# The down projection of a LUT feed-forward block in two parts of its contracted axis, with the partial rows kept in DRAM between them

## The chip, the cores and the metric

One core of one Trainium2 chip runs the whole program: a pre-norm block of attention over features and a feed-forward layer, in float32, on 2 x 2048 tokens of width 512. The metric is the device time of one execution in microseconds (us). The kernel before takes 1078.72 us (median of 3 runs, 1078.33 to 1079.13). The execution that the profiler recorded took 1078.93 us, and its instructions span 1077.2 us.

## The reference, cut to what matters

```python
x = x + attention(_layernorm(x), Wq, Wk, Wv, Wo)      # over the feature axis
x = x + ffn(_layernorm(x), lut, gate_idx, up_idx, down_idx)

def ffn(x, lut, gate_idx, up_idx, down_idx):          # HIDDEN 512, INTER 1376, LUT 16
    gate = einsum('bsh,oh->bso', x, lut[gate_idx])
    up = einsum('bsh,oh->bso', x, lut[up_idx])
    h = silu(gate) * up
    return einsum('bsh,oh->bso', h, lut[down_idx])
```

The weights of the feed-forward layer do not exist as numbers: each is an index from 0 to 15 into a table of 16 values, and the kernel has to look them up.

## The kernel before, in words

**Tiling.** The 4096 tokens are 8 chunks (NCH) of 512. The 1376 hidden features are 11 blocks (NFT), ten of 128 rows and one of 96. All large products go through a seven-product scheme (Strassen's, in Winograd's form): instead of eight products of half-size blocks, seven, for which VectorE first makes sums of the operands (S1, S2, S4 and S3 on one side, T1, T2, T4 and T3 on the other).

**Stages.** From 0 to about 295 us the program does the attention; from there to 804 us the gate and up products, in units of a block f and a pair of chunks p (`GateUp`), whose hidden rows go to DRAM (`hd`); from 804 us to the end the down products.

**Looking up.** A job (`Job`) turns a tile of 128x512 indices into weights on VectorE: four small operations on the bits of the index, eight `tensor_scalar` that pick between two table values (L278), and seven `copy_predicated` that merge them (L290). ScalarE first casts the indices to 16 bits (L252), and POOL loads them (L355 for down). There are 33 jobs, eleven each for gate, up and down. The list `jobs` has their order. They are not run in one go: `pump(us)` emits the next operations for about so many us, and the units call it through `between()` after each product, so that lookups and the rest of VectorE's work alternate. In the kernel before, all eleven down jobs are interleaved with the gate and up jobs and end before the last block of gate and up. Their results stay in one tile `wd`.

**between().** After each product of a unit, `between()` first takes an entry of the list `todo`, if there is one (sums to make, or other small work) and pumps 0.3 us of lookups; if there is none, it emits the sums that the next pair of blocks needs (`sums_left`, tiles `lc` and `lb`, as soon as its weights are there); otherwise it pumps `pace[0]` us.

**Down before.** For each chunk c, `Hidden(c)` loads all hidden rows of the chunk from DRAM: five pairs of blocks of 512 KB each (`h`, L1245) and the last block of 192 KB (`hr`, L1251), on SyncE's queue. VectorE makes the 21 sums of the chunk. Each chunk then has two units `Down(h, jj)`, for the two halves of its left rows. A unit has seven products: `a1`, `c1`, the `a4` of the unit before, `a2`, `c2`, `b`, `a3`; its own `a4` is the third product of the following unit. Each product adds up five pairs, and four of the seven also the last block: 39 matmuls of 128x256 a unit. After `a1`, `c1` and `a2` ScalarE copies the PSUM tile out (L1332, L1339, L1345), since the same PSUM tile is accumulated further; VectorE adds all seven results into rows `r` (L136). The rows start as the residual: the normed rows come back from DRAM (`xn_back`, two loads of 256 KB a unit, L1290) and ScalarE undoes the norm into `r` (`rows()`, two activations, L225). Finished rows are stored to the output.

**What sets the order around the change.** The order on PE, ScalarE, VectorE and SyncE is the order of the program's text; each engine runs its instructions in that order, and waits in it. Four orders matter. SyncE has, at the start of a chunk: the store of the last rows of the chunk before (L1362, which waits for VectorE's add after `a3`), then the loads of the next chunk's `h`, then the two `xn_back` loads for this chunk's second unit, then the store after `a4` (L1324). ScalarE has the two activations of L225 for a unit after the copies of the unit before and ahead of the unit's own copies. VectorE has, in the second unit of a chunk, the sums of the next chunk between the seven adds. PE's third product of a unit (`a4` of the unit before) needs the add after `a3`, its `a2` needs ScalarE's copy after `a1`.

Pools are stacks: `gub` (indices and lookup tiles) is released before the last block of gate and up, and the down tiles take its room.

Of the kernel before, what the change touches and what calls it, by code (L numbers as in the profile page):

```python
# [46 lines left out]
F32 = mybir.dt.float32  # L50
# [17 lines left out]
def tile_attn_ffn(  # L68
# [44 lines left out]
    lut_x = const.tile([P, NLUT // 2], I32, tag="lutx", name="lut_x")  # L113
    eps_sb = const.tile([P, 1], F32, tag="eps", name="eps_sb")
    lut_i = lut_sb.bitcast(I32)
    wd = wdp.tile([P, NFT, E], F32, tag="wd", name="wd")
    nd = dram.tile([NCH, P, KB, J, P], F32, tag="nd", name="nd")
    xnd = dram.tile([NCH, P, KB, J, P], F32, tag="xnd", name="xnd")
    hd = dram.tile([NCH, NFT, P, CH], F32, tag="hd", name="hd")


# [2 lines left out]
    def room(tag, name):  # L124
        return keep.tile([P, J, E], F32, tag=tag, name=name)
# [6 lines left out]
    def sub(dest, a, b):  # L132
        nc.vector.tensor_tensor(dest, a, b, ALU.subtract)
# [218 lines left out]
    def down_job(i):  # L352
        f0, rows = FT[i]
        return Job(
            f"wd{i}", rows, E, lambda queue, idx: queue.dma_start(idx, down_idx[f0 : f0 + rows, :]),  # L355
            lambda: wd[:rows, i, :], lambda: iter(()), lambda: True,
        )


    jobs = [job(f) for f in range(2) for job in (gate_job, up_job)]  # L360
    jobs += [down_job(i) for i in range(4)]
    for f in range(2, NFT - 1, 2):
        jobs += [gate_job(f), up_job(f), gate_job(f + 1), up_job(f + 1)]
        jobs += [down_job(i) for i in {2: (4,), 4: (5, 6), 6: (7,), 8: (8, 9)}[f]]
    jobs += [gate_job(NFT - 1), up_job(NFT - 1), down_job(NFT - 1)]
    assert len(jobs) == 3 * NFT

    def looked_up():
# [596 lines left out]
    def there(f):  # L965
        return f in gw and len(gw[f].shape) == 3 and f in uw
# [217 lines left out]
    todo = []  # L1184

    def between():
        if todo:
            todo.pop(0)()
            pump(0.3)
        elif sums_of and there(sums_of[0] | 1):  # L1190
            for op in sums_left(sums_of.pop()):
                op()
        else:
            pump(pace[0])

# [17 lines left out]
        late(i, **w)  # L1213


    wd_ops = []
    hps = {}

    def down_sums(pool):
        ops = []  # L1220
        for i in range(NPAIR):
            t = pool.tile([P, 3, H], F32, tag=f"t{i}", name=f"dT_{i}")
            t1, t2, t4 = (t[:, q, :] for q in range(3))
            b11, b12 = wd[:, 2 * i, :H], wd[:, 2 * i, H:]
            b21, b22 = wd[:, 2 * i + 1, :H], wd[:, 2 * i + 1, H:]
            wd_ops.append(
                {"11": b11, "T3": b12, "21": b21, "22": b22, "T1": t1, "T2": t2, "T4": t4}
            )
            ops += [
                lambda v=(t1, b12, b11): sub(*v), lambda v=(t2, b22, t1): sub(*v),  # L1230
                lambda v=(b12, b22, b12): sub(*v), lambda v=(t4, b21, t2): sub(*v),
            ]
        return ops

    class Hidden:


        ROOMS = [("a0", "x0", "a1"), ("a2", "a3", "x3")]

        def __init__(self, c):  # L1240
            self.c = c
            self.tiles = []
            for i in range(NPAIR):
                h = hps[c % 2].tile([P, 2, CH], F32, tag=f"h{i}", name=f"h_{c}_{i}")
                nc.sync.dma_start(h, hd[c, 2 * i : 2 * i + 2].rearrange("o p t -> p o t"))  # L1245
                self.tiles.append(h)

        def rest_of(self):
            c, rows = self.c, FT[NFT - 1][1]
            self.hr = hps[c % 2].tile([P, CH], F32, tag="hr", name=f"hr_{c}")[:rows]  # L1250
            nc.sync.dma_start(self.hr, hd[c, NFT - 1, :rows, :])  # L1251

        def sums(self):
            c, rows = self.c, FT[NFT - 1][1]
            places = []
            for tag in self.ROOMS[c % 2]:
                t = room(tag, f"hs_{c}_{tag}").rearrange("p j (q h) -> p (j q) h", h=H)
                places += [t[:, 0:3, :], t[:, 3:6, :]]
            self.pairs, ops = [], []
            for h, s in zip(self.tiles, places):  # L1260
                a11, a21 = h[:, 0, :H], h[:, 0, H:]
                a12, a22 = h[:, 1, :H], h[:, 1, H:]
                s1, s2, s4 = (s[:, q, :] for q in range(3))
                self.pairs.append(
                    {"11": a11, "12": a12, "S3": a21, "22": a22, "S1": s1, "S2": s2, "S4": s4}
                )
                ops += [
                    lambda v=(s1, a21, a22): add(*v), lambda v=(s2, s1, a11): sub(*v),
                    lambda v=(a21, a11, a21): sub(*v), lambda v=(s4, a12, s2): sub(*v),
                ]  # L1270
            h, s = self.hr, places[NPAIR][:rows, 0, :]
            self.rest = {"1": h[:, :H], "2": h[:, H:], "12": s}
            ops.append(lambda v=(s, h[:, :H], h[:, H:]): sub(*v))
            return ops

    class Down:


        def __init__(self, h, jj):
            self.h, self.c, self.jj, self.name = h, h.c, jj, f"{h.c}_{jj}"  # L1280
            self.r = []
            if h.c % 2 == 0 and jj == 0:
                for q in range(2):
                    rows_in[q] = room(f"x{1 + q}", f"r_{h.c}_{q}")
            if not normed_in:
                normed_in.append(room("sq0", "xn_back"))
            self.n = [normed_in[0][:, 2 * jj + i, :] for i in range(2)]
            self.n = [t.rearrange("p (i e) -> p i e", i=KB) for t in self.n]
            for i, j in enumerate((jj, 2 + jj)):
                nc.sync.dma_start(self.n[i], xnd[h.c][:, :, j, :])  # L1290
                self.r.append(rows_in[h.c % 2][:, 2 * jj + i, :])

        def rows(self):

            for i, j in enumerate((self.jj, 2 + self.jj)):
                ln2[self.c].undone(j, self.n[i], self.r[i])

        def at(self, a):
            return a[:, self.jj * P : (self.jj + 1) * P]

        def pairs(self, a, b):
            return [(self.at(self.h.pairs[i][a]), wd_ops[i][b]) for i in range(NPAIR)]

        def rest(self, a, b):
            rows = FT[NFT - 1][1]
            w = wd[:rows, NFT - 1, :]
            return [(self.at(self.h.rest[a]), w[:, :H] if b == "1" else w[:, H:])]

        def view(self, tag):
# [8 lines left out]

        def store_half(self, e):

            o, r = outr[self.c][:, self.jj, :], self.r[0]
            if self.c < NCH - 1 or self.jj == 0:
                if e:
                    nc.sync.dma_start(o, r)  # L1324
            else:
                nc.sync.dma_start(o[:, e * H : (e + 1) * H], r[:, e * H : (e + 1) * H])
# [31 lines left out]
        def a3(self):  # L1358

            mm(self.a, self.pairs("S1", "T1") + self.rest("2", "2"), False)  # L1360
            self.onto(1, 1, self.a)
            nc.sync.dma_start(outr[self.c][:, 2 + self.jj, :], self.r[1])  # L1362

        def a4(self):
            mm(self.a, self.pairs("S4", "22") + self.rest("12", "2"), False)
# [22 lines left out]
    for (f, p), following in zip(units, units[1:] + [(NFT, 0)]):  # L1388
# [8 lines left out]
        if f == NFT - 1 and p == 0:  # L1397
            assert not todo and next(lookup, None) is None
            x2p.release()
            gub.release()  # L1400
            for name in ("hp0", "dT"):
                hps[name] = tc.alloc_tile_pool(
                    name=name, bufs=1, side="right", reuse_waits="tile"
                )
            hps[0] = hps["hp0"]
            h = Hidden(0)
            todo += by_two(sums_last(f) + down_sums(hps["dT"]))
        if f == NFT - 1 and p == 1:
            h.rest_of()
            todo += by_two(h.sums())  # L1410
        if f == NFT - 1 and p == 3:
            units = [Down(h, 0)]
# [13 lines left out]
        op()  # L1426
    todo.clear()

    dtp = hps["dt"] = None
    for c in range(NCH):  # L1430
        nxt = None
        for jj in range(2):
            if c == 0 and jj == 0:
                units[0].rows()
                line.flush()
                ffn.release()
                wgu.release()
                hps[1] = tc.alloc_tile_pool(name="hp1", bufs=1, reuse_waits="tile")
                dtp = tc.alloc_tile_pool(name="dt", bufs=6, reuse_waits="tile")
            if jj == 0 and c + 1 < NCH:  # L1440
                nxt = Hidden(c + 1)
                nxt.rest_of()
            u = units.pop(0)
            if jj == 0:
                units.append(Down(h, 1))
            elif nxt is not None:
                units.append(Down(nxt, 0))
                todo += by_two(nxt.sums())
            line.run(u, final=nxt is None and jj == 1)
            if units:  # L1450
                units[0].rows()
        for op in todo:
            op()
        todo.clear()
        h = nxt
    line.flush()
    for pool in (dtp, hps[1], keep, hps["dT"], hps["hp0"]):
        pool.release()
    fps.release()

# [47 lines left out]
```

## Time and profile before

| stage (us from the start) | length | PE busy | VectorE busy | ScalarE busy | DMA |
|---|---|---|---|---|---|
| attention, to 295 | 295 | 291.6 | 244.1 | 138.0 | 42 to 272 GB/s |
| gate and up, 295 to 804 | 509 | 507.4 | 424.0 | 181.3 | 105 to 166 GB/s |
| down, 804 to the end | 273 | 269.6 | 99.8 | 41.2 | 134 GB/s |
| whole span 1077.2 | | 1068.6 (99%) | 768.0 (71%) | 360.5 (33%) | 143 GB/s |

The profiled execution took 1078.93 us for its span of 1077.2 us; 1.7 us lie outside. PE is TensorE's matmuls, PEld its weight loads, DVE VectorE, ACT ScalarE, SP SyncE; "SPq" in a row is a DMA being issued from SyncE. A matmul in float32 is recorded twice, so "x10" of PE is five matmuls. The timeline gives the start, the length, the instruction, and in brackets the idle time before it and what ended that.

### The profile page before, as it was taken

How to read it: one execution, taken by the hardware profiler on the slowest of the kernel's cores; microseconds unless marked ns; L12 is line 12 of the kernel's file. 1: busy time of each engine (PE TensorE's matmuls, PEld its weight loads, DVE VectorE, ACT ScalarE, POOL GpSimd, SP SyncE). 2: the span in 40 equal slices, each digit the busy share in tenths (PEclk: the TensorE clock that was granted, in tenths of full speed). 3: DMA queues.
4: the chain of work that ended last, by engine and by line, in shares of the span. 5: the costliest groups of instructions: out<-in, count | busy, mean ns of one | idle time of the engine just before them, and what ended most of it. 6: DMA issues, size and time to landing. Idle time of an engine off the chain costs nothing.

```text
span 1077.2 us, 10786 instructions
## 1 busy us (share of the span) xinstructions
PE 1068.6 (99%) x3426; PEld 641.0 (60%) x3426; DVE 768.0 (71%) x1660; ACT 360.5 (33%) x671; POOL 79.7 (7%) x118
## 2 busy tenths in 40 slices
PE   8999999999999999999999999999999999999998
PEld 5668886444444444444444444444348888888887
DVE  7878777889885889899899999985643334433341
ACT  4652432555632223333343343334221111111110
POOL 0000000011110000220120031012000000000000
PEclk9999999999999999999999999999999999999999
DMA  8750313589561244664574466456424545345421
GB/s 344 232 166 12 87 38 91 136 215 235 156 172 43 107 167 156 166 157 137 141 159 139 164 153 152 141 155 136 154 60 163 183 157 167 98 128 183 156 67 40
DMA packets 107769, 153.89 MB, mean 143 GB/s; under 512 B 16432, under 2 KB 52528, under 8 KB 106816
## 3 DMA queue, kind: packets, MB, share of 16 engines
q1 hardware_dynamic: 75744, 107.51, 30.6%
q0 software_dynamic: 11904, 28.91, 13.8%
q10 hardware_dynamic: 20064, 16.78, 4.9%
q8 instruction: 27, 0.44, 0.2%
q14 instruction: 30, 0.25, 0.1%
HBM read 89.73 MB, written 63.44 MB: 142 GB/s over the span
## 4 chain that ended last, share of the span: by engine, by line
PE 90%; DVE 4%; ACT 2%; DMA 1%; issue 1%; ACTq 1%; SPq 0%; DVEq 0%
PE a_g L997 27%; PE a_d L997 14%; PE y L770 10%; PE c_g L997 9%; PE c_d L997 7%; PE b_d L997 4%; PE x_g L997 4%; PE z_g L997 4%; PE b_g L997 2%; PE ea_t L607 1%; PE ea_p L607 1%; PE ea_m L607 1%; DVE st_a L154 1%; PE gp L454 1%; DMA x<-in_x_dram 1%
## 5 line engine op out<-in xcount | busy, mean ns | idle before, releaser
L770 PE MATMUL y<-m,nT 128*128 128x512 f32 x256 | 110.2, 592 | 0.0
L770 PEld LDWEIGHTS y<-m,nT 128*128 128x128 f32 x256 | 48.6, 190 | 60.4 <-issue 57.4
L997 PE MATMUL a_g<-xb,s 128*128 128x512 f32 (+1 forms) x176 | 82.7, 592 | 0.0
L997 PE MATMUL a_g<-xb,wg 128*128 128x512 f32 (+1 forms) x176 | 82.7, 592 | 0.0
L997 PE MATMUL c_g<-xb,wu 128*128 128x512 f32 (+1 forms) x176 | 82.7, 592 | 0.0
L997 PE MATMUL a_g<-xT_a,s 128*128 128x512 f32 (+1 forms) x176 | 82.7, 592 | 0.0
L454 PE MATMUL gp<-xn_a 128*128 128x128 f32 (+3 forms) x256 | 70.1, 434 | 1.7 <-DVE xn_a L177 0.9
L997 PE MATMUL a_g<-xT_sq,s 128*128 128x512 f32 (+1 forms) x132 | 62.0, 592 | 0.0
L454 PEld LDWEIGHTS gp<-xn_a 128*128 128x128 f32 x256 | 43.9, 190 | 28.5 <-issue 15.1
L997 PEld LDWEIGHTS a_g<-xb,s 128*128 128x128 f32 (+1 forms) x176 | 33.0, 188 | 42.5 <-issue 39.6
L997 PEld LDWEIGHTS a_g<-xT_a,s 128*128 128x128 f32 (+1 forms) x176 | 33.0, 188 | 42.5 <-issue 41.8
L997 PEld LDWEIGHTS c_g<-xb,wu 128*128 128x128 f32 (+1 forms) x176 | 33.0, 188 | 42.5 <-issue 42.3
L997 PEld LDWEIGHTS a_g<-xb,wg 128*128 128x128 f32 (+1 forms) x176 | 33.0, 188 | 42.5 <-issue 42.3
L290 DVE COPY_PREDICATED wd<-b_wd,wd 128x512 f32<-128x512 int16 (+1 forms) x77 | 56.4, 732 | 1.8
L997 PE MATMUL a_d<-dT,hs_a 128*128 128x256 f32 x224 | 56.2, 379 | 0.0
L136 DVE TENSOR_TENSOR r<-r,a_d 128x256 f32<-128x256 f32 x32 | 13.5, 421 | 53.7 <-PE a_d L997 53.7
L136 DVE TENSOR_TENSOR u<-c_g,u 128x512 f32<-128x512 f32 (+1 forms) x28 | 19.3, 690 | 37.5 <-PE c_g L997 31.7
L997 PEld LDWEIGHTS a_d<-dT,hs_a 128*128 128x128 f32 x224 | 42.4, 189 | 6.0
L278 DVE TENSOR_SCALAR wd<-idx_wd,lut_x,lut_sb 128x512 int32<-128x512 int32 (+1 forms) x88 | 44.5, 538 | 0.0
L997 PEld LDWEIGHTS a_g<-xT_sq,s 128*128 128x128 f32 (+1 forms) x132 | 24.8, 188 | 31.9 <-issue 31.4
L1128 ACT ACTIVATE h<-a_g 128x512 f32<-128x512 f32 (+1 forms) x44 | 26.2, 597 | 43.9 <-PE a_g L997 43.9
L1110 ACT ACTIVATE h<-h 128x512 f32<-128x512 f32 x24 | 15.1, 631 | 77.0 <-DVE h L136 77.0
(316 smaller groups left out, 2033.8 us busy)
## 6 DMA issues: line engine op xcount, KB each, us to landing
hd<-h SPq DMA_DIRECT2D x80, 256.0 KB, 2.2
h<-hd SPq DMA_DIRECT2D x40, 512.0 KB, 6.4
nl<-nd SPq DMA_DIRECT2D x32, 256.0 KB, 5.7
xnd<-xn_f ACTq DMA_DIRECT2D x16, 512.0 KB, 6.0
fl<-xnd POOLq DMA_DIRECT2D x32, 256.0 KB, 6.3
xn_back<-xnd SPq DMA_DIRECT2D x32, 256.0 KB, 4.4
out_dram<-r SPq DMA_DIRECT2D x31, 256.0 KB, 2.9
x<-in_x_dram SPq DMA_DIRECT2D x7, 1024.0 KB, 14.1
```

What stands on the lines that cost most here:

```text
L136: nc.vector.tensor_tensor(dest, a, b, ALU.add)
L154: nc.vector.bn_stats(st, block)
L278: vec.tensor_scalar(dest.bitcast(I32), idx, lut_x[:rows, k : k + 1], lut_i[:rows, at : at + 1], ALU.bitwise_and, ALU.bitwise_xor,)
L290: vec.copy_predicated(dest, masks[level - 1], t)
L454: nc.tensor.matmul(gp[b][i][:, i * P :], xn[:, i, j % 2, :], xn[:, i:, j % 2, :], start=c % CPB == 0 and j == 0, stop=c % CPB == CPB - 1 a ...
L607: nc.tensor.matmul(ps[:, m, :], self.a[a][:, k, m * P : (m + 1) * P], self.b[b][:, k, :], start=first and m == k == 0, stop=k == 1, skip_g ...
L770: nc.tensor.matmul(ys[k], nTs[k][:, i, :], m[:, i, :], start=(i == 0), stop=(i == KB - 1))
L997: nc.tensor.matmul(ps, lhsT, rhs, start=first and i == 0, stop=i == len(pairs) - 1, skip_group_check=not first,)
L1110: nc.scalar.activation(h0, self.p1 if self.role in (None, 3) else h0, AF.Silu)
L1128: nc.scalar.activation(self.h1, self.a, AF.Silu)
```

## The change

The down stage is run twice over all eight chunks. Part 0 takes the first three pairs of blocks of the contracted axis (K1 = 6 blocks), starts its rows from the residual as before, and stores the rows to a DRAM tensor `rd`. Part 1 takes the two other pairs and the last block, loads its rows from `rd` straight into `r`, and stores to the output. There are 32 units instead of 16: in part 0 a product adds up three matmuls (21 a unit), in part 1 two or three (18 a unit). The number of matmuls is the same; VectorE's adds grow from 112 to 224 and ScalarE's copies after `a1`, `c1`, `a2` from 48 to 96. The `h` loads are the same bytes in total, three pairs a chunk in part 0, two and `hr` in part 1.

The weights of the last five down blocks (6 to 10) get a tile `wd2` of their own, which exists only once the gate and up tiles are released. Their five jobs stand at the end of the list and run in part 0, pumped with `pace[0] = 0.75`; what is left of them would be emitted ahead of part 0's last chunk, where the sums of these weights are made too. `gub` stays until the end. Lookups in gate and up thus are five fewer, and the later gate and up jobs come earlier.

`between()` now emits `sums_left` before it takes from `todo`.

```diff
+    K1 = 6
+    wd = wdp.tile([P, K1, E], F32, tag="wd", name="wd")
+    rd = dram.tile([NCH, P, J, E], F32, tag="rd", name="rd")
...
-            lambda: wd[:rows, i, :], lambda: iter(()), lambda: True,
+            lambda: wd_block(i)[:rows], lambda: iter(()), lambda: i < K1 or wd2,
...
+    def wd_block(i):
+        return wd[:, i, :] if i < K1 else wd2[0][:, i - K1, :]
...
-        jobs += [down_job(i) for i in {2: (4,), 4: (5, 6), 6: (7,), 8: (8, 9)}[f]]
-    jobs += [gate_job(NFT - 1), up_job(NFT - 1), down_job(NFT - 1)]
+        jobs += [down_job(i) for i in {2: (4,), 4: (5,)}.get(f, ())]
+    jobs += [gate_job(NFT - 1), up_job(NFT - 1), *(down_job(i) for i in range(K1, NFT))]
...
     def between():
-        if todo:
+        if sums_of and there(sums_of[0] | 1):
+            for op in sums_left(sums_of.pop()):
+                op()
+        elif todo:
             todo.pop(0)()
             pump(0.3)
-        elif sums_of and there(sums_of[0] | 1):
-            for op in sums_left(sums_of.pop()):
-                op()
         else:
             pump(pace[0])
...
+    PARTS = [range(0, K1 // 2), range(K1 // 2, NPAIR)]
...
+            self.to = outr[h.c] if self.part else rd[h.c]
             for i, j in enumerate((jj, 2 + jj)):
-                nc.sync.dma_start(self.n[i], xnd[h.c][:, :, j, :])
                 self.r.append(rows_in[h.c % 2][:, 2 * jj + i, :])
+                if self.part:
+                    nc.sync.dma_start(self.r[i], rd[h.c][:, j, :])
+                else:
+                    nc.sync.dma_start(self.n[i], xnd[h.c][:, :, j, :])
...
-            for i, j in enumerate((self.jj, 2 + self.jj)):
+            for i, j in enumerate(() if self.part else (self.jj, 2 + self.jj)):
                 ln2[self.c].undone(j, self.n[i], self.r[i])
...
+    pace[0] = 0.75
+    parts = [(part, c) for part in range(2) for c in range(NCH)]
+    for (part, c), following in zip(parts, parts[1:] + [None]):
...
+                wdq = tc.alloc_tile_pool(name="wdq", bufs=1, reuse_waits="tile")
+                wd2.append(wdq.tile([P, NFT - K1, E], F32, tag="wd2", name="wd2"))
+            if (part, c, jj) == (0, NCH - 1, 0):
+                while step() is not None:
+                    pass
+                todo += by_two(down_sums(1, wdq))
+            if jj == 0 and following:
+                nxt = Hidden(*following)
                 nxt.rest_of()
```

More of the change, by code (lines that the diff above doesn't have):

```diff
@@ L115, in tile_attn_ffn @@
     lut_i = lut_sb.bitcast(I32)
-    wd = wdp.tile([P, NFT, E], F32, tag="wd", name="wd")
+    K1 = 6
+    wd = wdp.tile([P, K1, E], F32, tag="wd", name="wd")
     nd = dram.tile([NCH, P, KB, J, P], F32, tag="nd", name="nd")
     xnd = dram.tile([NCH, P, KB, J, P], F32, tag="xnd", name="xnd")
+    rd = dram.tile([NCH, P, J, E], F32, tag="rd", name="rd")
     hd = dram.tile([NCH, NFT, P, CH], F32, tag="hd", name="hd")
@@ L355, in down_job @@
             f"wd{i}", rows, E, lambda queue, idx: queue.dma_start(idx, down_idx[f0 : f0 + rows, :]),
-            lambda: wd[:rows, i, :], lambda: iter(()), lambda: True,
+            lambda: wd_block(i)[:rows], lambda: iter(()), lambda: i < K1 or wd2,
         )
+    wd2 = []
+    def wd_block(i):
+        return wd[:, i, :] if i < K1 else wd2[0][:, i - K1, :]
     jobs = [job(f) for f in range(2) for job in (gate_job, up_job)]
@@ L1213, in tile_attn_ffn, with down_sums @@
         late(i, **w)
-    wd_ops = []
+    wd_ops = {}
     hps = {}
-    def down_sums(pool):
+    PARTS = [range(0, K1 // 2), range(K1 // 2, NPAIR)]
+    def down_sums(part, pool):
         ops = []
-        for i in range(NPAIR):
+        for i in PARTS[part]:
             t = pool.tile([P, 3, H], F32, tag=f"t{i}", name=f"dT_{i}")
             t1, t2, t4 = (t[:, q, :] for q in range(3))
[L1224 to L1228, printed above, removed]
+            w1, w2 = wd_block(2 * i), wd_block(2 * i + 1)
+            b11, b12, b21, b22 = w1[:, :H], w1[:, H:], w2[:, :H], w2[:, H:]
+            wd_ops[i] = {"11": b11, "T3": b12, "21": b21, "22": b22, "T1": t1, "T2": t2, "T4": t4}
             ops += [
@@ L1235, in tile_attn_ffn, with __init__ @@
     class Hidden:
-        ROOMS = [("a0", "x0", "a1"), ("a2", "a3", "x3")]
-        def __init__(self, c):
-            self.c = c
+        ROOMS = [("a0", "x0"), ("a1", "a2")]
+        def __init__(self, part, c):
+            self.part, self.c, self.name = part, c, f"{part}_{c}"
             self.tiles = []
-            for i in range(NPAIR):
-                h = hps[c % 2].tile([P, 2, CH], F32, tag=f"h{i}", name=f"h_{c}_{i}")
+            for k, i in enumerate(PARTS[part]):
+                h = hps[c % 2].tile([P, 2, CH], F32, tag=f"h{k}", name=f"h_{c}_{i}")
                 nc.sync.dma_start(h, hd[c, 2 * i : 2 * i + 2].rearrange("o p t -> p o t"))
@@ L1249, in rest_of @@
             c, rows = self.c, FT[NFT - 1][1]
+            if not self.part:
+                return
             self.hr = hps[c % 2].tile([P, CH], F32, tag="hr", name=f"hr_{c}")[:rows]
@@ L1256, in sums @@
             for tag in self.ROOMS[c % 2]:
-                t = room(tag, f"hs_{c}_{tag}").rearrange("p j (q h) -> p (j q) h", h=H)
+                t = room(tag, f"hs_{self.name}_{tag}").rearrange("p j (q h) -> p (j q) h", h=H)
                 places += [t[:, 0:3, :], t[:, 3:6, :]]
-            self.pairs, ops = [], []
+            self.pairs, self.rest, ops = [], None, []
             for h, s in zip(self.tiles, places):
@@ L1270, in sums @@
                 ]
-            h, s = self.hr, places[NPAIR][:rows, 0, :]
-            self.rest = {"1": h[:, :H], "2": h[:, H:], "12": s}
-            ops.append(lambda v=(s, h[:, :H], h[:, H:]): sub(*v))
+            if self.part:
+                h, s = self.hr, places[len(self.tiles)][:rows, 0, :]
+                self.rest = {"1": h[:, :H], "2": h[:, H:], "12": s}
+                ops.append(lambda v=(s, h[:, :H], h[:, H:]): sub(*v))
             return ops
@@ L1279, in __init__ @@
         def __init__(self, h, jj):
-            self.h, self.c, self.jj, self.name = h, h.c, jj, f"{h.c}_{jj}"
+            self.h, self.c, self.jj, self.part = h, h.c, jj, h.part
+            self.name = f"{h.name}_{jj}"
             self.r = []
@@ L1283, in __init__ @@
                 for q in range(2):
-                    rows_in[q] = room(f"x{1 + q}", f"r_{h.c}_{q}")
+                    rows_in[q] = room(f"x{1 + q}", f"r_{h.name}_{q}")
             if not normed_in:
@@ L1288, in __init__ @@
             self.n = [t.rearrange("p (i e) -> p i e", i=KB) for t in self.n]
+            self.to = outr[h.c] if self.part else rd[h.c]
             for i, j in enumerate((jj, 2 + jj)):
-                nc.sync.dma_start(self.n[i], xnd[h.c][:, :, j, :])
                 self.r.append(rows_in[h.c % 2][:, 2 * jj + i, :])
+                if self.part:
+                    nc.sync.dma_start(self.r[i], rd[h.c][:, j, :])
+                else:
+                    nc.sync.dma_start(self.n[i], xnd[h.c][:, :, j, :])
         def rows(self):
-            for i, j in enumerate((self.jj, 2 + self.jj)):
+            for i, j in enumerate(() if self.part else (self.jj, 2 + self.jj)):
                 ln2[self.c].undone(j, self.n[i], self.r[i])
@@ L1301, in pairs @@
         def pairs(self, a, b):
-            return [(self.at(self.h.pairs[i][a]), wd_ops[i][b]) for i in range(NPAIR)]
+            return [
+                (self.at(h[a]), wd_ops[i][b]) for h, i in zip(self.h.pairs, PARTS[self.part])
+            ]
         def rest(self, a, b):
-            rows = FT[NFT - 1][1]
-            w = wd[:rows, NFT - 1, :]
+            if not self.part:
+                return []
+            w = wd_block(NFT - 1)[: FT[NFT - 1][1]]
             return [(self.at(self.h.rest[a]), w[:, :H] if b == "1" else w[:, H:])]
@@ L1319, in store_half @@
         def store_half(self, e):
-            o, r = outr[self.c][:, self.jj, :], self.r[0]
-            if self.c < NCH - 1 or self.jj == 0:
+            o, r = self.to[:, self.jj, :], self.r[0]
+            if self.c < NCH - 1 or self.jj == 0 or not self.part:
                 if e:
@@ L1361, in a3 @@
             self.onto(1, 1, self.a)
-            nc.sync.dma_start(outr[self.c][:, 2 + self.jj, :], self.r[1])
+            nc.sync.dma_start(self.to[:, 2 + self.jj, :], self.r[1])
         def a4(self):
@@ L1399, in tile_attn_ffn @@
             x2p.release()
-            gub.release()
             for name in ("hp0", "dT"):
@@ L1405, in tile_attn_ffn @@
             hps[0] = hps["hp0"]
-            h = Hidden(0)
-            todo += by_two(sums_last(f) + down_sums(hps["dT"]))
+            h = Hidden(0, 0)
+            todo += by_two(sums_last(f) + down_sums(0, hps["dT"]))
         if f == NFT - 1 and p == 1:
-            h.rest_of()
             todo += by_two(h.sums())
@@ L1427, in tile_attn_ffn @@
     todo.clear()
-    dtp = hps["dt"] = None
-    for c in range(NCH):
+    pace[0] = 0.75
+    parts = [(part, c) for part in range(2) for c in range(NCH)]
+    for (part, c), following in zip(parts, parts[1:] + [None]):
         nxt = None
         for jj in range(2):
-            if c == 0 and jj == 0:
+            if (part, c, jj) == (0, 0, 0):
                 units[0].rows()
@@ L1439, in tile_attn_ffn @@
                 dtp = tc.alloc_tile_pool(name="dt", bufs=6, reuse_waits="tile")
-            if jj == 0 and c + 1 < NCH:
-                nxt = Hidden(c + 1)
+                wdq = tc.alloc_tile_pool(name="wdq", bufs=1, reuse_waits="tile")
[6 more added lines that the diff above has]
+                nxt = Hidden(*following)
                 nxt.rest_of()
@@ L1456, in tile_attn_ffn @@
     line.flush()
-    for pool in (dtp, hps[1], keep, hps["dT"], hps["hp0"]):
+    for pool in (wdq, dtp, hps[1], keep, hps["dT"], hps["hp0"], gub):
         pool.release()
```

## The prediction

> **What bounds the kernel now.** I read the totals first, then busy time by stage, then PE's own waits, then one chunk of the down stage in order of time with the landing of its loads.
>
> ```profile
> PE 1068.6 (99%) x3426; PEld 641.0 (60%) x3426; DVE 768.0 (71%) x1660; ACT 360.5 (33%) x671; POOL 79.7 (7%) x118
> ```
>
> ```profile
> 380.00:420.00 40.00, 38.39 (x89) 16.47 (x88) 35.60 (x72) 12.37 (x22) 0.54 (x1) 1.00 0.49 166
> 420.00:804.00 384.00, 384.00 (x895) 166.19 (x894) 322.40 (x641) 143.76 (x252) 54.11 (x66) 1.00 0.54 145
> 804.00:1077.00 273.00, 269.64 (x1249) 236.54 (x1247) 99.81 (x260) 41.22 (x80) 0.00 (x0) 1.00 0.42 134
> ```
>
> ```profile
> PE z_g L997 <- DVE lc L133: 0.9, 1, 0.9
> PE z_g L997 <- ACT r_c L944: 0.7, 1, 0.7
> ```
>
> PE's work is the time. In each stretch the numbers are its length, then busy PE, PEld, DVE, ACT: gate and up hold 1.6 us without PE, both next to 395 us (the two waits), and the 3.4 us missing in down are the tail behind the last matmul. Relieving VectorE (84% in gate and up) can give back 1.6 us at most. [...]
>
> In down the chain has "c_d x10" (five matmuls) in 2.16 us: 0.432 us a matmul. 624 of them are 269.6 us, before and after; the split adds no PE work.
>
> ```profile
> 866.25 4.75 PE a_d L997 x22
> 871.00 2.16 PE c_d L997 x10
> ```
>
> ```profile
> 869.36 0.34 SPq L1362 DMA_DIRECT2D out_dram<-r  x1
> 869.79 2.60 SPq L1245 DMA_DIRECT2D h<-hd  x5
> 872.99 1.23 SPq L1290 DMA_DIRECT2D xn_back<-xnd  x2
> 881.21 1.62 ACT L225 ACTIVATE r<-xn_back,nmr_a,rstd_a 128x512 f32<-128x512 f32 x2 [2.88 <-DMA xn_back<-xnd]
> ```
>
> ```profile
> 888.29 0.43 DVE L136 TENSOR_TENSOR r<-r,p_d 128x256 f32<-128x256 f32 x1 [2.14 <-ACT p_d L1332]
> 888.64 0.42 DVE L136 TENSOR_TENSOR hs_a<-h 128x256 f32<-128x256 f32 x1
> 889.09 0.43 DVE L133 TENSOR_TENSOR hs_a<-hs_a,h 128x256 f32<-128x256 f32 x1
> ```
>
> The chunk's first unit began at 868.85 (866.25 + 6 x 0.432). Its loads issued at 869.79; `xn_back`, last in the burst, landed 11.4 us later, and ScalarE had stood waiting for it. That is harmless in a unit of 16.85 us. The change makes units of 9.07 us.
>
> **The change, part by part.**
>
> *Order in between().* At 382.9 us the eight small sums of `lc` and `lb` (394.59 to 396.46, 1.87 us) now precede the big T sums. The wait for `lc` (0.9) goes. Next late is the store `far_c1T`, for which VectorE idles: it issued at 384.32, now about 385.5, so after its 5.05 us at 390.5 instead of 389.4. From there to the `h` add took 7.07 us with the small sums in it, 5.2 without: 395.7 instead of 396.46. ScalarE's silu, copy and `r_c` hang on that add, and PE's second wait on `r_c`. Gain 0.75 us; bounds 1.6 (both waits) and a loss of 1.1 (the later store, passed on whole).
>
> *Five jobs leave gate and up.* PE never waited for a lookup there: nothing. The cover is that later weights come sooner.
>
> *Adds and copies.* 112 more adds and 48 more copies lie beside PE if VectorE keeps up. Start to start, VectorE needs 0.34 us an add, 1.47 for four sums (0.45 + 3 x 0.34), 0.46 for a pick and 0.62 for a merge. A job is 8 x 0.46 + 7 x 0.62 + 0.9 for the small ones, plus some 0.8 for dependent pairs: 9.7. A part-0 chunk holds 14 adds (4.8), 12 sums (4.4) and 7.8 us of pumped lookups (first unit 7 x 0.75; second, with six `todo` entries, 6 x 0.3 + 0.75): 17.0 of PE's 42 x 0.432 = 18.14 us. The five jobs (48 us) last six chunks, so nothing is left to be emitted in one go. VectorE has room on average, but not for waiting.
>
> ```profile
> 646.44 0.54 DVE L278 TENSOR_SCALAR u<-idx_u,lut_x,lut_sb 128x512 int32<-128x512 int32 x1
> 647.02 0.73 DVE L290 COPY_PREDICATED wu<-b_u,u 128x512 f32<-128x512 int16 x1
> 647.64 1.00 DVE L278 TENSOR_SCALAR u<-idx_u,lut_x,lut_sb 128x512 int32<-128x512 int32 x2
> ```
>
> *A loop of four queues in part 0.* Follow a chunk's second unit, in which VectorE is densest. From its first add to its `a3` add VectorE now has seven adds, twelve sums, two picks and a merge (8.4 us on average by the order of the changed kernel), 8.1 to the start of the last. Behind that add waits SyncE: store, then the next loads, 0.9 us (885.73 add, 886.22 store, 886.62 loads). Then three `h` loads and two `xn_back`, 2.1 MB, must land: D. ScalarE undoes the second row block (0.75) and only then copies the next `a1`, for which VectorE's first add waits (0.4). The loop closes after 8.1 + 0.9 + D + 1.15, against PE's 18.14; it makes PE wait if D is over 8.0.
>
> *D* is not in the trace as such. The fourth `h` load of the seven bursts completes the same 2.1 MB. It landed 8.2, 8.4, 8.5, 9.0, 9.0, 10.2 and 10.8 us after the first issue (two of these rows, from 871.4 and 1006.8 us):
>
> ```profile
> h<-hd SPq DMA_DIRECT2D x1, 512.0 KB, 6.7
> ...
> h<-hd SPq DMA_DIRECT2D x1, 512.0 KB, 8.6
> ```
>
> I take the median, 9.0, and keep 8.2 and 10.8. [...]
>
> With D = 9.0 the loop takes 19.1 us, 1.0 too long, six times (first to seventh chunk, while lookups last or their lateness does): 6.0 us. The start: loads at 805.9, so the second unit's first add at 805.9 + 9.0 + 1.15 = 816.1; that unit starts at 803.87 + 18 x 0.432 = 811.65, so 4.45 us in. PE's `a2` needs the copy by 3.9 us: 0.6 more. Part 0 costs 6.6 us, as ScalarE waits, then `a4` and `a2` on PE. At D = 8.2 it is 0.2 x 6 and 0.4 for the first `a3` add (due 11.65 us into the unit, done 12.0): 1.6; at 10.8 it is 2.8 x 6 + 2.4 = 19.
>
> *Part 1.* No lookups; a chunk's second unit has 7 adds and 9 sums (5.7 us), the rows come without ScalarE, and 1.76 MB must land (about 7.5 us, from the third and fourth landings): 5.7 + 0.6 + 7.5 + 0.1 = 13.9 us against 36 x 0.432 = 15.55. Hidden. If that cover went (loads as slow as the slowest burst, 9.5), the loop would be 15.9, 0.35 x 7 = 2.5 us. `rd` was written long before; its bytes replace those of `xn_back`, its stores those of the output. SyncE issues 48 more DMAs at 0.35 to 0.65 us beside PE.
>
> *Late waits of `a4`.* It comes 2.6 us after `a3` ends (1.7 in part 1, before 4.3). The add is normally done 0.7 after; counted above where it is later.
>
> [...]
>
> Sum: 1078.93 (profiled) - 0.75 + 6.6 = 1084.8; the median is 0.2 lower, so **1084.6 us**.
>
> **Rivals.**
> - *The loop stays covered* (not slower). Place: `xn_back` in part 0's first units. If the burst lands in 8.0 us or less, nothing accumulates: 1078.7 - 0.75 + 0.2 = 1078.2. For it: five loads queue for less time than eight, and the first `h` lands after only 3.9 us. Against: ScalarE already waits 30.6 us for this load, and SyncE's issue gets later.
> - *The slow bursts rule.* Two of seven took 10.2 or more; if stores to `rd` and index loads make that the rule: 19 us, 1097.
> - *VectorE itself is the bound*: if waits between dependent operations cost 10% more than counted, 18.7 against 18.14 a chunk, 0.6 x 6 = 3.4 us even with quick loads: 1081.4. Against: the starts above already hold the dependent spacing.
> - *The relief works in gate and up after all*: both waits go and part 0 is covered: 1077.1. Even so it stays inside 0.2% (2.2 us, about what a measurement here can tell from no change).
>
> **How the numbers follow.** Loop as priced, D about 8.5 to 10: 0.50. Covered, or D near 8.2 (1079.6): 0.22. Slow bursts: 0.13. VectorE bound: 0.10. Relief: 0.05. Slower: the first, the third and the fourth, and a little of the second, 0.75; same: the rest of the second and part of the last, 0.22; faster by over 0.2%: 0.03, should the relief be worth more than the two waits. The range leaves out the relief and most of the slow bursts: 1078.0 to 1091.0; the likeliest case alone is 1081.5 to 1090.
>
> **What would show it.** Right: PE's waits in part 0 name DVE `r` or ACT `p_d`; ScalarE waits for `xn_back` in the first units and VectorE for `p_d` in the second, growing later chunk by chunk up to the seventh; chunk periods near 19 us there, 18.1 in the eighth, 15.55 in part 1; the wait for `lc` gone and the one for `r_c` left. Wrong: bursts landing within 8 us; waits in part 1 for `r<-rd`; a shorter gate and up by more than 1.6 us.

## The result and the profile after

The changed kernel takes **1088.99 us** (median of 4 runs, 1087.36 to 1089.79) against 1078.53 us before (4 runs beside them, 1078.21 to 1079.13): ratio 1.0094, 95% interval 1.0077 to 1.0112. It is slower by 10.5 us; the forecast was 1084.6, range 1078 to 1091. The loss was right in kind and in place and 4.4 us short in size.

The profiled execution of the changed kernel took 1089.62 us, its span 1087.8 (before 1078.93 and 1077.2), so the profile carries the loss: 10.7 us, or 10.6 by the spans. Totals of the changed kernel, busy us of each engine:

```profile
PE 1074.4 (99%) x3426; PEld 641.3 (59%) x3426; DVE 805.3 (74%) x1772; ACT 378.4 (35%) x719; POOL 79.8 (7%) x118
```

As many matmuls as before, and more work on VectorE and ScalarE. PE's total rose by 5.8 us for the same matmuls, so part of what it lost is booked as busy time, and 99% says nothing of the rest. Its time by stage does (length, then busy PE, PEld, DVE, ACT and POOL, then PE's granted clock, DMA share, GB/s):

```profile
380.00:420.00 40.00, 40.00 (x95) 17.59 (x94) 38.54 (x77) 13.21 (x23) 1.08 (x2) 1.00 0.50 172
420.00:804.00 384.00, 384.00 (x901) 167.14 (x900) 268.38 (x527) 142.97 (x249) 51.92 (x62) 1.00 0.54 140
804.00:1088.00 284.00, 272.75 (x1238) 234.54 (x1236) 188.21 (x482) 58.99 (x129) 1.66 (x3) 0.99 0.64 194
```

Between 380 and 420 us the 1.6 us without PE are gone. In the rest of gate and up VectorE now works 54 us less and PE gains nothing from it: it was full and stays full. In the down stage there are now 11.2 us without PE, where there were 3.4. PE's waits from 375 us on (what PE waited for: us in total, times, longest):

```profile
PE a_d L1006 <- ACT p_d L1351: 5.9, 6, 2.1
PE a_d L1006 <- DVE r L140: 1.1, 3, 0.6
PE c_d L1006 <- DVE h L137: 0.2, 1, 0.2
```

The two waits on `lc` and `r_c` have left the list, and ScalarE's copy of `a` and VectorE's adds, the end of the forecast loop, have come onto it. In the chain of work that ended last, PE fell from 90% to 86% and DMAs rose from 1% to 5% (kernel before first):

```profile
PE 90%; DVE 4%; ACT 2%; DMA 1%; issue 1%; ACTq 1%; SPq 0%; DVEq 0%
```

```profile
PE 86%; DVE 5%; DMA 5%; ACT 2%; issue 1%; SPq 0%; ACTq 0%; DVEq 0%
```

One turn of the loop, from the timeline of the changed kernel (start, duration, engine, instruction, and in brackets what the engine waited for just before):

```profile
842.64 0.33 SPq L1381 DMA_DIRECT2D rd<-r  x1
843.06 2.61 SPq L1253 DMA_DIRECT2D h<-hd  x3
845.72 1.46 SPq L1307 DMA_DIRECT2D xn_back<-xnd  x2
...
853.43 1.61 ACT L229 ACTIVATE r<-xn_back,nmr_a,rstd_a 128x512 f32<-128x512 f32 x2 [7.53 <-DMA xn_back<-xnd]
...
855.33 0.43 DVE L140 TENSOR_TENSOR r<-r,p_d 128x256 f32<-128x256 f32 x1 [4.85 <-ACT p_d L1351]
855.35 1.13 PE L1006 MATMUL a_d<-dT,hs_a 128*128 128x256 f32 x4 [2.09 <-ACT p_d L1351]
...
863.26 0.41 DVE L140 TENSOR_TENSOR r<-r,a_d 128x256 f32<-128x256 f32 x1
863.74 0.33 SPq L1381 DMA_DIRECT2D rd<-r  x1
864.16 1.44 SPq L1253 DMA_DIRECT2D h<-hd  x3
```

Read it downwards: SyncE issues the burst at 843.06; the second `xn_back` has landed by 854.2, when the second undo starts (an undo takes 0.81 us, and that row ends at 855.04; D = 11.2 us); the copy frees `a`, and VectorE's first add starts at 855.33 (1.1 later) with PE's `a2` beside it; VectorE reaches the `a3` add at 863.26 (7.9); SyncE, which stood behind that add, stores at 863.74 and issues the next burst at 864.16 (0.9). That is 21.1 us for work of which PE's share is 18.14. ScalarE waited 7.53 us and VectorE 4.85 us in a chunk that is late: neither is short of time, both wait for the burst.

The eight bursts of part 0 left 19.1, 20.2, 21.1, 19.9, 19.1, 21.0 and 17.8 us apart. From part 0's first down matmul (801.62) to part 1's (958.13) PE took 156.5 us for 333 matmuls, whose own time is 143.8 (143.74 and 143.87 in two runs below in which PE does not wait there): **12.7 us lost in part 0**. The first of them comes 2.25 us earlier than before (803.87), and what follows part 1's first matmul takes some 0.2 longer than its matmuls and the old tail together: -2.25 + 12.7 + 0.2 = 10.65.

### The profile page after: what moved, and what is told of

It reads as the page before. It is cut to its first block, busy times and chain, and to the rows that moved or that the text cites. A ratio compares the mean times of both kernels' runs of the same rounds, so it can differ in the third digit from the quotient of the medians.

```text
span 1087.8 us, 11146 instructions
## 1 busy us (share of the span) xinstructions
PE 1074.4 (99%) x3426; PEld 641.3 (59%) x3426; DVE 805.3 (74%) x1772; ACT 378.4 (35%) x719; POOL 79.8 (7%) x118
## 4 chain that ended last, share of the span: by engine, by line
PE 86%; DVE 5%; DMA 5%; ACT 2%; issue 1%; SPq 0%; ACTq 0%; DVEq 0%
PE a_g L1006 28%; PE y L779 10%; PE c_g L1006 9%; PE a_d L1006 9%; DMA xn_back<-xnd 5%; PE gp L463 4%; PE c_d L1006 4%; PE x_g L1006 4%; PE z_g L1006 4%; PE b_g L1006 3%; PE b_d L1006 2%; PE ea_t L616 1%; PE ea_p L616 1%; PE ea_m L616 1%; DVE r L140 1%
## 5 line engine op out<-in xcount | busy, mean ns | idle before, releaser
L1006 PE MATMUL a_d<-dT,hs_a 128*128 128x256 f32 x288 | 73.2, 381 | 5.9 <-ACT p_d L1351 5.9
L1006 PEld LDWEIGHTS a_d<-dT,hs_a 128*128 128x128 f32 x288 | 54.0, 189 | 15.7 <-ACT p_d L1351 8.3
L140 DVE TENSOR_TENSOR r<-r,p_d 128x256 f32<-128x256 f32 x64 | 26.9, 422 | 43.2 <-ACT p_d L1351 36.4
L1140 DVE TENSOR_TENSOR h<-h,c 128x512 f32<-128x512 f32 (+1 forms) x44 | 30.0, 683 | 21.7 <-ACT h L1137 21.6
L1351 ACT COPY p_d<-a_d 128x256 f32<-128x256 f32 x32 | 11.8, 367 | 94.2 <-PE a_d L1006 94.2
```

Source lines behind the costliest of these rows:

```text
L140: nc.vector.tensor_tensor(dest, a, b, ALU.add)
L1006: nc.tensor.matmul(ps, lhsT, rhs, start=first and i == 0, stop=i == len(pairs) - 1, skip_group_check=not first,)
L1140: nc.vector.tensor_tensor(self.h1, self.h1, self.c22, ALU.mult)
L1351: nc.scalar.copy(p1, self.a)
```

## The experiments

All times are medians; the kernel before, run on the same chip between them, took 1078.7 us in the first four runs and 1078.8 in the last four.

**The order in between() by itself**: the kernel before, with only this edit.

```diff
     def between():
-        if todo:
+        if sums_of and there(sums_of[0] | 1):
+            for op in sums_left(sums_of.pop()):
+                op()
+        elif todo:
             todo.pop(0)()
             pump(0.3)
-        elif sums_of and there(sums_of[0] | 1):
-            for op in sums_left(sums_of.pop()):
-                op()
```

> The kernel before with nothing but the new order in between(). The profile of the changed kernel has its first down matmul 2.25 us earlier, 2.15 us of it between 380 and 400 us, where the small sums now come first. If the order alone does that: 1076.3 us (before, 1078.5, less 2.15), with the waits for lc and r_c both gone. If the forecast's sizing was right and something else gave the rest: 1077.8 (less 0.75). If the five jobs that leave gate and up gave it (relief): 1078.5, no change.

Measured: 1076.63 us (1076.37 to 1077.33), ratio 0.9982 [0.9973, 0.9991]: 2.07 us faster. PE has no wait left after 375 us. The timeline shows what the forecast had missed:

```profile
385.51 2.59 SPq L899 DMA_DIRECT2D far_c1T<-T_c  x3
389.31 0.69 DVE L133 TENSOR_TENSOR T_b<-xb,xb 128x512 f32<-128x512 f32 x1 [1.56 <-DMA far_c1T<-T_c]
394.24 1.02 PE L997 MATMUL z_g<-T_c_in,lc 128*128 128x512 f32 x2
394.51 0.68 DVE L136 TENSOR_TENSOR h<-b_g,h 128x512 f32<-128x512 f32 x1
```

The store left at 385.51, as forecast (385.5), and the way from `T_b` to the `h` add took 5.2 us, as forecast. But the store landed after 3.8 us and not after the 5.05 that it had taken before, so the `h` add came at 394.5 instead of the forecast 395.7, and `r_c` was in time too. That landing scatters: in the other profiles with the new order it took 2.8 to 4.4 us, and 4.8 in the one with the old order. In the two with the new order in which it took over 4 us (the rows first, and the lookups in the first unit, both below) PE waited for `r_c` again, 0.5 and 0.2 us. The whole gain of the change is this order, and the kernel before with nothing but it is faster than both the kernel before and the changed one.

**The other way round**: the changed kernel with the old order.

```diff
     def between():
-        if sums_of and there(sums_of[0] | 1):
-            for op in sums_left(sums_of.pop()):
-                op()
-        elif todo:
+        if todo:
             todo.pop(0)()
             pump(0.3)
+        elif sums_of and there(sums_of[0] | 1):
+            for op in sums_left(sums_of.pop()):
+                op()
```

> The changed kernel with the old order in between(). By the order of the sums: 1091.1 us (1089.0 plus 2.15), both waits near 395 us back. By relief: 1089.0, since the five jobs still run in the down stage.

Measured: 1089.87 us (4 runs, 1088.71 to 1090.56). The two waits are back:

```profile
PE z_g L1006 <- ACT r_c L953: 0.7, 1, 0.7
PE z_g L1006 <- DVE lc L137: 0.6, 1, 0.6
```

In its profile the first down matmul starts at 803.26 us, 1.6 later than in the changed kernel. The sign is as expected. The median rose by 0.9 only, but both kernels scatter over 2 us, and in these two profiles part 0 lost 10.8 and 12.7 us; this run doesn't size the gain, the one before does.

**The rows first**: the decisive one. The same loads on the same queue, the two `xn_back` loads ahead of the three `h` loads (and in part 1, by the same lines, the two loads from `rd` ahead of its `h` loads).

```diff
-            if jj == 0 and following:
+            if jj == 0:
+                units.append(Down(h, 1))
+            if jj == 0 and following:
                 nxt = Hidden(*following)
                 nxt.rest_of()
             u = units.pop(0)
             if jj == 0:
-                units.append(Down(h, 1))
+                pass
             elif nxt is not None:
```

> The changed kernel with the two xn_back loads of a chunk's second unit issued ahead of the three h loads instead of behind them. Theory (a loop of four queues, closed by the landing of the last load of the burst, 10.0 us on average): the undo then waits for 0.5 MB, about 4 to 5 us after the first issue, so the loop closes in 8.1 + 0.9 + 4.5 + 1.15 = 14.7 us, under PE's 18.14, and part 0's periods fall to 18.1; 11.0 us of waiting go, and with PE's long wait the clock dip of 1.7 us: 1076.3 to 1077.5 us. Rival 'VectorE itself is the bound': nothing moves, 1089. Rival 'the transfers of the split are too slow as such' (the h loads, now last, are late for the sums instead): 1083 or more, with VectorE waiting for h.

Measured: 1077.00 us (1076.72 to 1077.72), ratio to before 0.9984 [0.9976, 0.9993]: 12 us less than the changed kernel, and under the kernel before. From 800 to 960 us, changed kernel first, then this one:

```profile
800.00:960.00 160.00, 152.59 (x680) 128.77 (x679) 123.01 (x310) 44.34 (x87) 1.66 (x3) 0.99 0.62 187
```

```profile
800.00:960.00 160.00, 160.00 (x737) 139.36 (x736) 131.22 (x329) 47.46 (x92) 1.65 (x3) 1.00 0.65 203
```

In the same 160 us VectorE does 8 us *more* and the DMAs move more bytes a second, and PE has no gap. Part 0 takes 143.87 us, 333 matmuls at 0.432. So over these 160 us neither VectorE (123.01 and 131.22 us busy) nor the transfers (a share of 0.62 and 0.65) were full; only the order made the last landing late. ScalarE's wait for the rows, in the changed kernel and here:

```profile
ACT r L229 <- DMA xn_back<-xnd: 48.2, 12, 7.5
```

```profile
ACT r L229 <- DMA xn_back<-xnd: 7.9, 10, 1.6
```

The rivals "VectorE itself is the bound" (1089 expected here) and "the transfers of the split are too slow as such" fall.

**The split without the move of the lookups**: all eleven blocks looked up in gate and up, with `wd` whole and `gub` released as before the change.

```diff
-        jobs += [down_job(i) for i in {2: (4,), 4: (5,)}.get(f, ())]
-    jobs += [gate_job(NFT - 1), up_job(NFT - 1), *(down_job(i) for i in range(K1, NFT))]
+        jobs += [down_job(i) for i in {2: (4,), 4: (5, 6), 6: (7,), 8: (8, 9)}[f]]
+    jobs += [gate_job(NFT - 1), up_job(NFT - 1), down_job(NFT - 1)]
```

> The split of K with rows through DRAM kept and the new order in between() kept, but all eleven blocks of down's weights looked up in gate and up, as before. The loop theory: two picks and a merge (1.5 us) leave the second unit, so the loop takes 20.15 - 1.5 = 18.6 us against 18.14, 0.5 x 6 and 0.6 at the start, 3.4 us instead of 11.0, without the clock dip of 1.7 us: 1079.7 us, 1081.4 if the dip stays; ScalarE still waits for xn_back. If VectorE's load alone were the bound: no wait in part 0, 1076.3. If the lookups had no part in it: 1089. Should relief have given the 2.15 us in gate and up, 2.15 comes on top.

Measured: 1078.49 us, with a wide scatter for 11 runs (1077.65 to 1080.64). In the profile:

```profile
PE a_d L1006 <- ACT p_d L1351: 0.8, 2, 0.4
ACT r L229 <- DMA xn_back<-xnd: 37.6, 10, 5.8
```

ScalarE still waits 37.6 us for the rows, so the late landing is still there, but part 0 loses only 1.3 us. D, read as above, was 9.0 to 10.4 us, 9.5 on average against 10.0: with the picks gone the loop takes 8.1 - 1.5 + 0.9 + 9.5 + 1.15 = 18.15 us against 18.14. It stands on its threshold, which fits the scatter. The expectation was 1.2 us too high because it had left D at 10.0. What shortens D here was not isolated. The index loads, which fall away, can be a small part of it at most: in the changed kernel's trace two of POOL's three were in flight during a burst (844.13 to 850.2 and 868.15 to 875.5), and D averaged 10.5 us in these two and 9.8 in the four others, which makes 0.2 of the 0.5 us.

**The store behind the loads**: in part 0 the store after the second unit's `a3`, for which SyncE waits, goes behind the five loads.

```diff
-            nc.sync.dma_start(self.to[:, 2 + self.jj, :], self.r[1])
+            if self.part or not self.jj:
+                nc.sync.dma_start(self.to[:, 2 + self.jj, :], self.r[1])
+            else:
+                stores.append((self.to[:, 2 + self.jj, :], self.r[1]))
...
                 units.append(Down(h, 1))
+                if stores:
+                    nc.sync.dma_start(*stores.pop())
```

> The changed kernel with one store moved on SyncE's queue: in part 0 the store of a chunk's second unit after a3 is issued behind the five loads that follow it instead of ahead of them. It cuts the loop at another place than the run with the rows first: the loads no longer wait for VectorE's a3 add (8.1 + 0.9 us leave the loop), and the landing D stays 10 us or so. Loop theory: part 0 at PE's pace, 1076.6 to 1077.6 us, like the run with the rows first (1077.0). If only the order of the transfers mattered (the rows standing behind 1.5 MB of h), nothing is gained: 1089. VectorE as the bound: 1089 as well.

Measured: 1078.19 us (1078.05 to 1078.87), 10.8 us under the changed kernel, with the order of the loads untouched. So the loop can be opened at SyncE as well as at the landing. It is 0.6 us above the expected range, and the starts of PE's `a1` show where (the lines between them left out):

```profile
809.97 1.46 PE L1006 MATMUL a_d<-wd,h 128*128 128x256 f32 x6
...
814.69 1.13 PE L1006 MATMUL a_d<-dT,hs_a 128*128 128x256 f32 x4 [0.67 <-ACT p_d L1351]
...
819.98 1.46 PE L1006 MATMUL a_d<-wd,h 128*128 128x256 f32 x6
...
829.64 1.46 PE L1006 MATMUL a_d<-wd,h 128*128 128x256 f32 x6
...
838.71 1.46 PE L1006 MATMUL a_d<-wd,h 128*128 128x256 f32 x6
```

Units of 10.01, 9.66 and then 9.07 us: after the first chunk PE runs at its own pace, and the first chunk costs 0.94 + 0.60 = 1.5 us. Its burst had no store ahead of it, so this edit can't help it. The changed kernel has the same two late units (9.90 and 9.68). This measures the forecast's separate term for the start by itself.

**One load more**: 256 KB into a tile that nobody reads, ahead of the `xn_back` loads.

```diff
                 else:
+                    if self.jj and not i:
+                        t = room("x3", f"more_{self.name}")
+                        nc.sync.dma_start(t[:, 0, :].rearrange("p (i e) -> p i e", i=KB), xnd[h.c][:, :, j, :])
                     nc.sync.dma_start(self.n[i], xnd[h.c][:, :, j, :])
```

> The changed kernel with one load more of 256 KB in each of part 0's bursts, between the h loads and the xn_back loads of the second unit, into a tile that nobody reads. Loop theory: D grows by 256 KB's share, (10.0 - 3.9) us over the last 1.6 MB of the burst, about 1.0 us, and each of the six periods with it: 1089.0 + 6 x 1.0 = 1095 us, more if PE's longer waits bring more dips of its clock (1.7 us each). If the transfer had slack, or VectorE were the bound: 1089.

Measured: 1094.93 us (1094.59 to 1097.79), 5.9 us above the changed kernel, where 6 were expected. In the two profiles the difference is 5.0 us, and part 0's seven periods are 5.1 us longer in all. A longer burst goes straight to the end, as only a loop without slack does. PE's waits for the copy grow to

```profile
PE a_d L1006 <- ACT p_d L1354: 10.7, 7, 2.4
```

**The lookups in the first unit only**: as many a chunk, none between the second unit's first add and its `a3` add.

```diff
             todo.pop(0)()
-            pump(0.3)
-        else:
+            if pace[0]:
+                pump(0.3)
+        elif pace[0]:
             pump(pace[0])
...
             u = units.pop(0)
+            pace[0] = 0.0 if jj else 1.11
```

> The changed kernel with the lookups of part 0 pumped only in a chunk's first unit (pace 1.11 instead of 0.75) and not at all in its second; as many lookups a chunk (7.8 us) and the same loads. VectorE does the same work, but the 1.5 us of it that lay between the second unit's first add and its a3 add leave the loop: 20.15 - 1.5 = 18.65 against 18.14. Loop theory: 0.5 x 6 + 0.6 of waiting instead of 11.0, without the dip: 1080 us (1079 to 1082). If VectorE's total were the bound, the place of its work would not matter: 1089.

Measured: 1081.13 us (1079.87 to 1082.90), 7.9 us less than the changed kernel for the same work of VectorE; 9 were expected. VectorE's term is in the loop by its place; its total alone does not set the time. The profiled execution, the fastest of ten (1079.87), lost 2.5 us in part 0, nearly all in one new wait,

```profile
PE a_d L1006 <- DVE r L140: 2.3, 1, 2.3
```

at the first chunk's `a4`: the denser first unit now makes the add before it late. The bursts left 17.95 to 18.74 us apart, on the threshold again; what the slower executions lost beyond this stays open, as only this one has a trace.

**Split, rows first, all lookups in gate and up**: the two edits together.

```diff
-        jobs += [down_job(i) for i in {2: (4,), 4: (5,)}.get(f, ())]
+        jobs += [down_job(i) for i in {2: (4,), 4: (5, 6), 6: (7,), 8: (8, 9)}[f]]
...
+            if jj == 0:
+                units.append(Down(h, 1))
             if jj == 0 and following:
                 nxt = Hidden(*following)
```

> The split with all lookups in gate and up and with the rows loaded first: the last corner. If the move of five lookups out of gate and up is worth nothing once the loop is open, as the forecast has it: the same as the run with lookups in the down stage and the rows first, 1077.0 us (within 0.4). If the relief of VectorE in gate and up is worth something there: above 1077.5. The split itself then costs this time less that of the kernel before with the new order alone, 1076.6: some 0.4 us.

Measured: 1076.82 us (1076.61 to 1077.53). PE waits for nothing after 375 us, and part 0 takes 143.74 us. Against the run with the lookups moved (1077.00) it is 0.2 us faster, against the order alone without any split (1076.63) 0.2 slower; executions of one of these kernels differ by 0.9 to 1.0 us. With the loop open, moving five lookups out of gate and up brings nothing, and splitting K costs next to nothing.

## Why the prediction was right, and where it was short

- *PE bounds the kernel, and the split adds no work to it*: right. With the rows first part 0 takes 333 matmuls times 0.432 us and no more. The relief of VectorE is worth nothing (1077.00 us with it, 1076.82 without). In gate and up the full PE row was the limit (from 420 to 804 us PE was busy 384.00 of 384.00 us, with VectorE busy 322.40 before and 268.38 after). In part 0 it was not: there PE's busy time took in some of what it lost.
- *Order in between()*: the step was right in what follows what, and mis-sized: 0.75 us forecast, 2.07 measured, past its upper bound of 1.6. The step that failed is the landing of `far_c1T`, carried over as 5.05 us from the trace before; it was 3.8 in the run with the order alone, and 2.8 in the changed kernel, so the wait on `r_c` went as well. And in the profiles of the kernel before and of this run the first down matmul moved by 1.95 us (803.87 to 801.92), where the two waits were listed at 1.6: the list leaves out some 0.3 us around them.
- *Five jobs leave gate and up: nothing*: right (the last run, without their move, is 0.2 us faster).
- *VectorE has room on average, but not for waiting*: right on both counts. It did more per us when the rows came first, and with the same total 7.9 us went when its lookups moved within the chunk.
- *The loop of four queues*: right as a mechanism. It was cut at the landing (-12.0 us), at SyncE's queue (-10.8) and shortened on VectorE (-7.9), and lengthened by a dose of 256 KB (+5.9); each term answered. Three of its terms measured as forecast in the chunk shown: 7.9 for 8.1, 0.9 for 0.9, 1.1 for 1.15.
- *D = 9.0 us* is the mis-sized term. Read from the second undo's start, the first six bursts took 9.2, 10.3, 11.2, 9.8, 9.3 and 10.5 us, 10.0 on average; the loop comes to 20.15 us by the forecast's other terms, and its mean period was 20.1. PE lost 11.2 us to it instead of 6.0. The forecast took D from the fourth `h` loads of the bursts before, the same bytes but not the same loads (from the issue times in the trace these seven took 8.2 to 10.5 us, median 8.9: the forecast's longest, 10.8, is 0.3 too long, its median right to 0.1). In the two longest bursts SyncE's own issue of the three `h` loads took 2.61 and 3.35 us instead of the usual 1.45. What made it longer, and D with it, stays open. Index loads met two of the bursts, but the four others averaged 9.8 us too.
- *The start, 0.6 us*: 1.5 measured. The forecast followed the late copy to `a2`; that listed wait is as forecast (0.57 us), but the unit grew by 0.83, and the next one by another 0.6.
- *Part 1 hidden*: right. Its first bursts leave 15.55 to 15.57 us apart, PE's pace, and PE has no listed wait in it.
- *The sum*: 1078.93 - 0.75 + 6.6 was forecast for the profiled execution, and -2.25 + 1.5 + 11.2 + 0.2 makes 1089.6 against its 1089.62. Two errors of opposite sign, 1.5 us too little gain and 6.3 too little loss, leave 4.8 there, and 4.4 between the forecast and the median: that the forecast is no further off is in part luck.
- *Rivals*: "the loop stays covered" and "VectorE itself is the bound" fell. So did "the relief works in gate and up": both waits went, as it had said, but by the order in `between()`. Of "the slow bursts rule" half came true: D stayed under the 10.8 that it was priced at in all bursts but one, but above the median before.

## What to carry to other kernels

When the busiest engine's own work hides a loop over several queues, add up one turn of the loop before halving the units: every load in the turn counts with the landing of the *last* transfer of its burst. Put first in the burst what a waiting engine needs first; here two lines' order was worth 12 us, more than the whole change cost. A landing time taken from another burst should enter the sum with its whole range when the loop has no slack, since each tenth of a us is paid once a turn: here the median of the bursts before (9.0) was 1.0 us too low and their longest as read there (10.8) 0.8 too high.

## What the runs showed of the hardware

**After a wait of 2.09 us PE's granted clock fell to 0.50.** In the changed kernel PE waited 2.09 us, to 855.35; from 856 to 860 us, while it was at work, its granted clock (the third number from the end) was under 1.00:

```profile
856.00:857.00 1.00, 1.00 (x6) 0.82 (x5) 0.96 (x4) 0.00 (x0) 0.00 (x0) 0.76 0.13 38
857.00:858.00 1.00, 1.00 (x4) 0.81 (x3) 1.00 (x5) 0.79 (x3) 0.00 (x0) 0.50 0.00 0
858.00:859.00 1.00, 1.00 (x4) 0.81 (x3) 0.97 (x4) 1.00 (x3) 0.00 (x0) 0.50 0.00 0
859.00:860.00 1.00, 1.00 (x4) 0.73 (x4) 1.00 (x4) 0.52 (x1) 0.00 (x0) 0.54 0.70 262
```

The shortfall is 0.24 + 0.50 + 0.50 + 0.46 = 1.7 us. With one load more PE waited 2.42 us, to 836.11, and its clock was 0.50 from 837 to 840 us (0.94 in the us before, 0.85 in the us after). With the lookups in the first unit it waited 2.27 us, to 814.90, and the clock was 1.00 in every stretch of 5 us from 800 to 960. So two of three waits of 2.1 to 2.4 us were followed by a fall. No run moved a wait on purpose: what decides whether the clock falls was not shown.

**The dip itself cost nothing that the trace shows.** The expectations above priced it at 1.7 us. But from VectorE's first add to SyncE's store the chunk with the dip took 8.41 us (855.33 to 863.74), and the chunk before it, without one, 8.41 too (834.23 to 842.64): PE only had less to wait in the next chunk (its units from 862.32 to 880.45 run at 9.07). While a loop outside PE set the pace, the slower PE was hidden. This is one dip beside one chunk without; no run removed the dip alone.
